# Start of a two-layer Fourier-filter network: filter weights in four pieces, the store of u in the next tick, image rows a tick earlier

## The chip, the cores and the metric

One Trainium2 chip, one of its cores. The metric is the device time of one execution in microseconds. The kernel before took 4927.3 us (median of three runs, 4927.09 to 4930.28).

## What is computed

Eight images of 128 x 128 points with 96 channels go through two layers. A layer is a convolution by Fourier transform, followed by a small network on every point.

```
x_pre = relu(x @ w1.T)**2 * scale + bias              # 96 -> 192 channels
xf    = rfft2(x_pre)                                  # over height and width
filt  = three small complex filters cw0, cw1, cw2, each enlarged
        to 128 x 65 by a matrix Rh on the left and Rw on the right
r     = softmax over the three filters, from means of x (one set per image)
xff   = xf * sum(filt * r)
xsp   = irfft2(xff) @ w2.T                            # 192 -> 96 channels
y     = feed-forward 96 -> 384 -> 96 with fp8 products, on each point
```

Two things matter here. The filters depend on the weights alone: the enlargement by Rw is done once per layer, early in the kernel, and its result `u` is kept in DRAM (`u_d`). The rest is done for every image.

## The kernel before

The program is written for one core and is entirely ordered by hand. Work is cut into generators: `pixels` (stage P, 21 steps) takes a group of eight image rows from load to width transform and stores it to `a_d`; `frequencies` (F, 19 steps) takes four columns of the spectrum, loads `al` from `a_d` and `ut` from `u_d`, makes the filter for the image (POOL multiplies `ut` by the gate, L703; PE makes `pf`, L715), multiplies and transforms back to `y_d`; `tokens` (S) does the rest and the feed-forward. `filters` (U) makes one of twelve parts of `u` for a layer; `Norms.steps` (N) finishes the statistics of normalisation; `gate` (G) computes the softmax of one image.

A tick is one pass over a list of triples (stage, step, ahead). In tick t the triple makes the named step for group t + ahead, less the offset of the stage. The order of a list is the order in which instructions stand on each engine. RAMP serves the ticks before 15, when only rows are worked on and the filters of layer 1 are made; RISE serves ticks 15 to 35, when spectra are worked on as well, and the filters of layer 2 are made in ticks 21 to 32; TICK serves the long steady part, FALL and TAIL the end. All DMAs are issued by SyncE (SP) in the order of the list, and SP waits for each one's inputs before it goes to the next.

What the change touches:

- `load_filters` (L279) issues the load of the filter weights `cw` of one layer, in four pieces of 26 partitions x 4608 values (468 KB each). It is called in `background`, a generator that advances by one yield per tick, after step 9 of P. For layer 1 that is in tick 0, for layer 2 in tick 17.
- `token_weights` (L408) loads and casts the feed-forward weights; `background` runs it for layer 1 in ticks 12 to 16.
- `filters` (L285) has three steps: four matmuls with `rw` (L292); two copies on ACT (L305); two copies on DVE (L307) together with the store of `u` to `u_d` (L311, 390 KB).
- `pixels` step 0 (L541 to L544) loads a group's rows into `xt` by four DMAs of 96 KB; step 1 takes its statistics on DVE (`st`, L483) and step 2 normalises it on POOL (`xn_a`, L554), which is the last reader. Three `xt` buffers rotate. In RAMP step 0 and step 1 both stand at ahead 4: a group is loaded in the tick in which its statistics are taken. In RISE and TICK the load stands at 3 and the statistics at 2.
- `padding` writes zeros between the halves of `u_d` (780 KB), in tick 11 for layer 1.
- RISE_GATE holds, by place in RISE, where gate steps are put in.

Shorter rows of names used below: `at` (L612, L613) is the width transform's result, stored to `a_d` at L616, 768 KB a tick; `xT` (L561) is the transposed group; `sd` (L587), `pa` (L596), `r` (L572), `xs` (L575) are steps between.

Of the kernel before, what the change touches and what calls it, by code (L numbers as in the profile page):

```python
# [10 lines left out]
F32 = mybir.dt.float32  # L11
# [8 lines left out]
B, H, W, C = 8, 128, 128, 96  # L20
# [53 lines left out]
}  # L74

RISE = (
    ("F", 7, 1), ("P", 1, 2), ("P", 0, 3), ("P", 13, -1), ("U", 0, 0), ("F", 12, 0),
    ("P", 3, 1), ("P", 5, 0), ("N", 0, 0), ("U", 1, 0), ("P", 4, 1), ("F", 13, 0),
    ("U", 2, 0), ("P", 14, -1), ("P", 6, 0), ("P", 15, -1), ("F", 8, 1), ("P", 16, -1),
    ("P", 17, -1), ("F", 14, 0), ("P", 7, 0), ("P", 18, -1), ("F", 9, 1), ("P", 8, 0),  # L80
# [20 lines left out]
)  # L101

RAMP = (
    ("U", 0, 0), ("P", 0, 4), ("P", 13, 0), ("U", 1, 0), ("P", 20, -1), ("P", 7, 1),
    ("P", 1, 4), ("U", 2, 0), ("P", 3, 2), ("P", 4, 2), ("P", 8, 1), ("N", 1, -1),
    ("P", 14, 0), ("N", 0, 0), ("N", 2, -1), ("P", 2, 3), ("P", 9, 1), ("P", 10, 1),
    ("P", 15, 0), ("P", 11, 1), ("P", 16, 0), ("P", 17, 0), ("P", 18, 0), ("P", 19, 0),
# [119 lines left out]
def _bc(ap, n):  # L227

    p, a = ap.shape
    return ap.unsqueeze(2).to_broadcast([p, a, n])  # L230
# [9 lines left out]
def metaformer_kernel(ctx: ExitStack, tc: tile.TileContext, x, cst, layers, out):  # L240
# [10 lines left out]
    def bank2(name):  # L251
        return pp.tile([128, 2, 512], F32, name=name, tag=f"d{banks[name]}")

    def bank1(name):
        return pp.tile([128, 512], F32, name=name, tag=f"s{banks[name]}")
# [23 lines left out]
    def load_filters(l, p):  # L279

        cws[l] = us.tile([128, UM, NG], F32, name="cw")
        for i in range(M // UM):
            nc.sync.dma_start(cws[l][32 * i : 32 * i + NWS], p["cw"][:, i * UM : (i + 1) * UM, :])

    def filters(i):  # L285

        l, n0 = i // NU, i % NU * UN
        pu = bank2("ps_u")
        pss = [pu[:NKW, i, : UN * UM] for i in range(2)]
        pss += [bank1(f"ps_v{i}")[:NKW, : UN * UM] for i in range(2)]  # L290
        for i in range(M // UM):
            mm(  # L292
                pss[i].rearrange("p (n m) -> p n m", m=UM),
                kt["rw"][32 * i : 32 * i + NWS],
                cws[l][32 * i : 32 * i + NWS, :, n0 : n0 + UN].rearrange("p m n -> p n m"),
                start=True,
                stop=True,
            )
        yield
        u = us.tile([NKW, UN, M], F32, name="u", bufs=3)  # L300
        uv = u.rearrange("p n (i m) -> p i n m", m=UM)
        for i, ps in enumerate(pss):
            o = ps.rearrange("p (n m) -> p n m", m=UM)
            if i < 2:
                nc.scalar.copy(uv[:, i], o)  # L305
            else:
                nc.vector.tensor_copy(uv[:, i], o)  # L307
            if i == 1:
                yield
        n1 = n0 if n0 < NHS else 64 + n0 - NHS  # L310
        nc.sync.dma_start(u_d[l][:, n1 : n1 + UN, :], u)  # L311
        yield
# [9 lines left out]
    def load(l, name, shape, view):  # L322
        temps[l][name] = us.tile(shape, F32, name=name)
        nc.sync.dma_start(temps[l][name], view)
        return temps[l][name]

    def kept(l, name, shape, dtype=F32):
        wts[l][name] = const.tile(shape, dtype, name=f"{name}_{l}")
        return wts[l][name]
# [78 lines left out]
    def token_weights(l, p):  # L408
        wt = wts[l]
        f1 = load(l, "f1_f", [C, HID], p["ffn_W1"])  # L410
        yield
        f2 = load(
            l, "f2_f", [128, HID // 128, C], p["ffn_W2"].rearrange("(k p) c -> p k c", p=128)
        )
        yield
        b1 = load(l, "b1_f", [128, HID // 128], p["ffn_b1"].rearrange("(k p) -> p k", p=128))
        b2 = load(l, "b2_f", [128, C], p["ffn_b2"].partition_broadcast(128))
        yield
        yield
        for name, t in (("f1", f1), ("f2", f2), ("b1", b1), ("b2", b2)):  # L420
            nc.vector.tensor_copy(kept(l, f"{name}_q", list(t.shape), F8), t, saturate=False)
        nc.vector.tensor_copy(kept(l, "b1", [128, HID // 128]), wt["b1_q"])
        nc.vector.tensor_copy(kept(l, "b2", [128, C], F16), wt["b2_q"])
        yield

    def background():

        load_filters(0, layers[0])
        constants("rw")
        yield  # L430
        yield from other_weights(0, layers[0])
        for k in ("fwd", "rh"), ("inv", "rh0"), ("fwd0", "inv0"), ("idft",):
            constants(*k)
            yield
        padding(0)
        yield
        yield from token_weights(0, layers[0])
        load_filters(1, layers[1])
        yield
        yield from projection_weights(1, layers[1])  # L440
        yield from other_weights(1, layers[1])
        yield from token_weights(1, layers[1])
# [14 lines left out]
    ab = ctx.enter_context(tc.tile_pool(name="ab", bufs=2))  # L457
# [79 lines left out]
    def pixels(jb, g):  # L537
        wt = jb.wt


        xt = ab.tile([128, 2, 2, 2 * C], F32, name="xt", bufs=3)  # L541
        for p in range(2):
            for a in range(2):
                nc.sync.dma_start(xt[64 * p : 64 * p + 64, a], pixel_rows(jb.src, g, p, a))  # L544
        yield
        if g == 0:
            jb.gs = ab.tile([C, NRG], F32, name="gs")
            jb.acc = ab.tile([128, 4, SC], F32, name="acc")
        xt = xt.rearrange("p a s (j c) -> p (a s j) c", c=C)
        nm = norms[-1].stats(0, xt)  # L550
        yield
        rs = nm.rs[:, 0]
        xn = ab.tile([128, RG, C], F32, name="xn_a")
        nc.gpsimd.tensor_tensor(xn, xt, _bc(rs, C), ALU.mult)  # L554
        yield
        pt = bank2("pt_a").rearrange("p a (r t) -> p (a r) t", t=128)[:C]
        for j in range(RG):
            nc.tensor.transpose(pt[:, j, :], xn[:, j, :], ident)  # L558
        yield
        xT = xTs[g % 2]  # L560
        nc.scalar.activation(xT[:C], pt, AF.Copy, accum_out=jb.gs[:, g : g + 1])  # L561
        yield
        sds = []
        for j in range(2):
            pw = bank2(f"pw{j}")[:, :, : 2 * WE]
            for a in range(2):
                for i in range(2):
                    o = pw[:, a, i * WE : (i + 1) * WE]
                    mm(o, xT[:, 4 * a + 2 * i + j, :], wt["w1"], start=True, stop=True)  # L569
            yield  # L570
            r = ab.tile([128, 2, 2, WE], F32, name="r")
            nc.scalar.activation(r.rearrange("p a s c -> p a (s c)"), pw, AF.Relu)  # L572
            yield
            xs = ab.tile([128, 2, 2, M], F32, name="xs")
            nc.scalar.activation(xs, r[:, :, :, :M], AF.Square)  # L575
            yield
            rc = r[:, :, :, M:].rearrange("p a s c -> p (a s) c")
            if g == 0 and j == 0:
                nc.gpsimd.tensor_copy(jb.acc, rc)
            else:  # L580
                nc.gpsimd.tensor_tensor(jb.acc, jb.acc, rc, ALU.add)  # L581
            yield

            sd = ab.tile([128, 2, 2, M], F32, name="sd")
            for e, op in enumerate((ALU.add, ALU.subtract)):
                on = nc.gpsimd if (j, e) in on_pool["sd"] else nc.vector
                on.tensor_tensor(sd[:, e], xs[:, 0], xs[:, 1], op)  # L587
            sds.append(sd)
            yield
        pas = []  # L590
        for j, sd in enumerate(sds):

            pa = bank2(f"pa{j}")[:, :, : 2 * M]
            for p in range(2):
                for e in range(2):
                    mm(  # L596
                        pa[64 * e : 64 * e + 64, p].rearrange("q (s m) -> q s m", m=M),
                        wt["dft"][64 * p : 64 * p + 64, 64 * e : 64 * e + 64],
                        sd[64 * p : 64 * p + 64, e],
                        start=True,  # L600
                        stop=True,
                    )
            pas.append(pa.rearrange("q p (s m) -> q p s m", m=M))
            yield

        at = ab.tile([128, RH, 2, M], F32, name="at")
        av = at.rearrange("q (p j) e m -> q p j e m", j=2)
        for j, pa in enumerate(pas):
            lo = ab.tile([128, 2, M], F32, name="lo")
            nc.scalar.copy(lo, pa[:, :, 1, :])  # L610
            yield
            nc.vector.tensor_tensor(av[:, :, j, 0, :], pa[:, :, 0, :], lo, ALU.add)  # L612
            nc.vector.tensor_tensor(av[:, :, j, 1, :], pa[:, :, 0, :], lo, ALU.subtract)  # L613
            if j == 0:
                yield
        nc.sync.dma_start(jb.a[:, g * RH : (g + 1) * RH], at)  # L616
        yield
# [388 lines left out]
    with tc.manual_schedule():  # L1006
# [5 lines left out]
        for t in range(-first, n + offset["S"] + behind + 1):  # L1012
# [23 lines left out]
            for place, (stage, step, ahead) in enumerate(order):  # L1036
                for gate_step, image in gates.get(place, ()):
                    advance("G", gate_step, image)
                i = t - offset[stage] + ahead
# [45 lines left out]
```

## Time and profile before

| | |
|---|---|
| median of the runs | 4927.3 us |
| profiled execution | 4929.2 us, span 4927.4 us, mean TensorE clock 0.986 |
| busy over the span | PE 4813.4, DVE 4592.9, ACT 4311.3, PE weight loads 3751.1, POOL 2532.6 us |
| DMA | 1020.97 MB, 207 GB/s |

The page gives the busy time of each engine over the whole span. The matmul time of PE is modelled, so a full PE is not a PE at its peak. The slices are 123 us long, longer than the whole ramp has dips; for a change at the start they have to be cut finer, with the table by stretches of time, whose columns are the length, the busy time of PE, PE weight loads, DVE, ACT and POOL (with counts), the granted clock, the DMA share and GB/s. In a list of waits, the three numbers are microseconds in total, how often, and the longest. In a timeline, a row has its start, its length, engine, line and operation; in brackets stands the idle time before it and what ended it.

### The profile page before, as it was taken

The numbers are of one execution on the slowest core, as the hardware profiler recorded it, in microseconds if no ns is written. First come the engines' busy times: TensorE is split into PE (matmuls) and PEld (weight loads), VectorE is DVE, ScalarE is ACT, GpSimd is POOL, SyncE is SP. The second block draws the span as 40 slices with busy tenths as digits, with TensorE's granted clock in tenths as the row PEclk, the third lists the DMA queues.
The fourth block names the chain that finished last, engine by engine and source line by source line (L and its number), as shares of the span: only waits on it lengthen the run. The fifth ranks groups of instructions, "written<-read, shape, count | busy, mean of one in ns | idle before, by whom it ended". The sixth has DMA issues, their size and how long they took to land.

```text
span 4927.4 us, 124008 instructions
## 1 busy us (share of the span) xinstructions
PE 4813.4 (98%) x44232; PEld 3751.1 (76%) x44232; DVE 4592.9 (93%) x13949; ACT 4311.3 (87%) x7104; POOL 2532.6 (51%) x1886
## 2 busy tenths in 40 slices
PE   7899999999999999999999999999999999999987
PEld 4677777777778777777777777777777877777763
DVE  7788999999999999999999999999999999998998
ACT  6555899999999999999999999999999999998987
POOL 4445455555555555555555555555555555554544
PEclk9899999999999999999999999999999999999997
DMA  5667777777777777777777777777777777776754
GB/s 174 189 196 196 208 213 217 215 213 214 213 215 217 213 215 212 219 208 219 212 216 213 214 214 213 217 216 214 214 212 215 219 211 215 211 218 182 204 168 126
DMA packets 917425, 1020.97 MB, mean 207 GB/s; under 512 B 75826, under 2 KB 848914, under 8 KB 916602
## 3 DMA queue, kind: packets, MB, share of 16 engines
q1 hardware_dynamic: 916810, 1013.04, 73.8%
q8 instruction: 353, 5.78, 0.5%
q14 instruction: 262, 2.15, 0.1%
HBM read 598.92 MB, written 413.84 MB: 206 GB/s over the span
## 4 chain that ended last, share of the span: by engine, by line
PE 88%; DVE 5%; ACT 4%; issue 1%; DMA 1%; SPq 1%; POOL 0%; POOLq 0%; DVEq 0%; ACTq 0%
PE pw L569 16%; PE py L749 14%; PE pz L839 8%; PE pf L715 7%; PE pa L596 7%; PE pi L855 7%; PE pm L934 6%; PE pz L831 5%; PE po L951 5%; PE pt_a L558 4%; PE ps_r L889 4%; PE pt_c L924 2%; DVE st L483 1%; ACT y L937 1%; ACT xn_c L910 1%
## 5 line engine op out<-in xcount | busy, mean ns | idle before, releaser
L792 POOL TENSOR_TENSOR xf<-pr 128x768 f32<-128x768 f32 x512 | 930.9, 1818 | 427.1 <-DVE pr L777 413.8
L569 PE MATMUL pw<-w,xT 97*128 97x240 f32 x4096 | 944.3, 374 | 7.4 <-DVE at L613 2.9
L749 PE MATMUL py<-k_fwd,al 128*128 128x128 f32 (+1 forms) x6208 | 801.9, 280 | 0.0
L937 ACT CAST y<-pm 128x1024 f16<-128x1024 f32 x768 | 754.8, 1017 | 42.8 <-PE pm L934 42.6
L569 PEld LDWEIGHTS pw<-w,xT 97*128 97x128 f32 x4096 | 742.5, 191 | 61.6 <-ACT r L572 7.4
L749 PEld LDWEIGHTS py<-k_fwd,al 128*128 128x128 f32 (+1 forms) x6208 | 744.5, 191 | 41.1 <-DVE pr L777 3.1
L944 ACT ACTIVATE h<-a 128x1024 fp8e5<-128x1024 f16 x729 | 773.1, 1061 | 0.2 <-DVE a L940 0.2
L969 POOL TENSOR_TENSOR y<-xr,o 128x768 f32<-128x768 f32 x256 | 421.9, 1648 | 674.1 <-DVE o L966 601.1
L581 POOL TENSOR_TENSOR acc<-acc,r 128x192 f32<-128x192 f32 x496 | 295.6, 596 | 919.5 <-ACT r L572 840.1
L572 ACT ACTIVATE r<-pw 128x960 f32<-128x960 f32 x512 | 496.9, 970 | 132.5 <-PE pw L569 131.2
L773 DVE TENSOR_TENSOR pr<-py,cf 128x768 f32<-128x768 f32 x512 | 486.3, 950 | 54.9 <-PE py L749 42.0
L587 DVE TENSOR_TENSOR sd<-xs 128x384 f32<-128x384 f32 x1008 | 518.7, 554 | 1.7 <-PE pa L596 1.4
L703 POOL TENSOR_TENSOR ut<-ut,rw 112x768 f32<-112x768 f32 (+1 forms) x256 | 473.2, 1849 | 49.8 <-DMA ut<-u_d 37.4
L715 PEld LDWEIGHTS pf<-k_rh,ut 48*128 48x128 f32 x6080 | 362.5, 189 | 159.4 <-issue 142.4
L934 PE MATMUL pm<-xq,f_q 96*128 96x512 fp8e5 x1536 | 431.9, 390 | 32.2 <-ACT y L937 25.2
L554 POOL TENSOR_TENSOR xn_a<-xt,n_rs 128x768 f32<-128x768 f32 x256 | 380.9, 1488 | 145.9 <-DVE n_rs L517 126.5
L927 ACT ACTIVATE xq<-pt_c 96x1024 fp8e5<-96x1024 f32 x256 | 260.7, 1018 | 202.8 <-PE pt_c L924 202.7
L575 ACT ACTIVATE xs<-r 128x768 f32<-128x768 f32 x512 | 436.6, 853 | 0.6 <-POOL sd L587 0.2
L715 PE MATMUL pf<-k_rh,ut 48*128 48x128 f32 x6080 | 412.4, 282 | 13.8 <-POOL ut L703 11.0
L910 ACT ACTIVATE xn_c<-xr,n_nb,n_rs 128x96 fp8e5<-128x96 f32 x1058 | 413.1, 488 | 0.0
L596 PE MATMUL pa<-sd,dft 64*64 64x384 f32 x4096 | 393.9, 496 | 8.9 <-DVE sd L587 6.2
L756 ACT COPY cf<-pf 128x768 f32<-128x768 f32 x496 | 372.7, 801 | 33.6 <-PE pf L715 33.2
(133 smaller groups left out, 10156.6 us busy)
## 6 DMA issues: line engine op xcount, KB each, us to landing
a_d<-at SPq DMA_DIRECT2D x256, 768.0 KB
al<-a_d SPq DMA_DIRECT2D x1024, 192.0 KB
y_d<-yt SPq DMA_DIRECT2D x512, 192.0 KB
v<-y_d SPq DMA_DIRECT2D x256, 384.0 KB
ut<-u_d SPq DMA_DIRECT2D x256, 336.0 KB
xt<-in_x_dram SPq DMA_DIRECT2D x512, 96.0 KB
xr<-in_x_dram SPq DMA_DIRECT2D x256, 192.0 KB
mid<-y SPq DMA_DIRECT2D x256, 192.0 KB
```

The source lines that it names most:

```text
L569: mm(o, xT[:, 4 * a + 2 * i + j, :], wt["w1"], start=True, stop=True)
L572: nc.scalar.activation(r.rearrange("p a s c -> p a (s c)"), pw, AF.Relu)
L587: on.tensor_tensor(sd[:, e], xs[:, 0], xs[:, 1], op)
L596: mm(pa[64 * e : 64 * e + 64, p].rearrange("q (s m) -> q s m", m=M), wt["dft"][64 * p : 64 * p + 64, 64 * e : 64 * e + 64], sd[64 * p : 64 ...
L703: nc.gpsimd.tensor_tensor(ut[:, -n:], ut[:, -n:], _bc_mid(jb.rw, n), ALU.mult)
L715: mm(pf[:, i, t * 128 : (t + 1) * 128], utf[64 * i : 64 * i + NHS, c0 : c0 + 128], kt["rh"][64 * i : 64 * i + NHS, :], start=True, stop=True,)
L749: mm(py[p0:p1, t, e, :], alf[:, e, c0 + p0 : c0 + p1], f, start=True, stop=True)
L773: nc.vector.tensor_tensor(p0, yv, crb, ALU.mult)
L792: nc.gpsimd.tensor_tensor(xf.rearrange("p t e f -> p (t e) f"), pr[:, 0].rearrange("p t r k -> p t (r k)"), pr[:, 1].rearrange("p t r k -> ...
L934: mm(pm[:, s, :], fk, xq[:, s, :], start=True, stop=True)
L937: nc.scalar.copy(y16, pm)
L944: nc.scalar.activation(hk, a16, AF.Copy, saturate=False)
```

## The change

The load of layer 2's `cw` yields between its four pieces. `background` starts it in the fourth step of layer 1's `token_weights`, so pieces are issued in ticks 15, 16, 17 and 18; layer 1's four pieces still go in one tick. What follows in `background` comes one tick later. The store of `u` becomes a fourth step of `filters`, which RAMP and RISE run as their first entry for the part of the tick before. RAMP loads rows at ahead 5 instead of 4, and `xt` has four buffers. As the first tick is numbered by the largest ahead in RAMP, the loop starts one tick earlier; that tick issues nothing.

```diff
 RISE = (
-    ("F", 7, 1), ("P", 1, 2), ("P", 0, 3), ("P", 13, -1), ("U", 0, 0), ("F", 12, 0),
+    ("U", 3, -1),    ("F", 7, 1), ("P", 1, 2), ("P", 0, 3), ("P", 13, -1), ("U", 0, 0), ("F", 12, 0),
...
 RAMP = (
-    ("U", 0, 0), ("P", 0, 4), ("P", 13, 0), ("U", 1, 0), ("P", 20, -1), ("P", 7, 1),
+    ("U", 3, -1), ("U", 0, 0), ("P", 0, 5), ("P", 13, 0), ("U", 1, 0), ("P", 20, -1), ("P", 7, 1),
...
         for i in range(M // UM):
+            if l and i:
+                yield
             nc.sync.dma_start(cws[l][32 * i : 32 * i + NWS], p["cw"][:, i * UM : (i + 1) * UM, :])
...
             if i == 1:
                 yield
+        yield
         n1 = n0 if n0 < NHS else 64 + n0 - NHS
         nc.sync.dma_start(u_d[l][:, n1 : n1 + UN, :], u)
...
-        load_filters(0, layers[0])
+        yield from load_filters(0, layers[0])
...
-        yield from token_weights(0, layers[0])
-        load_filters(1, layers[1])
+        cw1 = load_filters(1, layers[1])
+        for k, _ in enumerate(token_weights(0, layers[0])):
+            if k >= 3:
+                next(cw1)
+            yield
+        for _ in cw1:
+            yield
         yield
...
-        xt = ab.tile([128, 2, 2, 2 * C], F32, name="xt", bufs=3)
+        xt = ab.tile([128, 2, 2, 2 * C], F32, name="xt", bufs=4)
```

## The prediction

> **What bounds the kernel now.** I read the page's slices first, to see which stretches are not full.
>
> ```profile
> PE   7899999999999999999999999999999999999987
> PEclk9899999999999999999999999999999999999997
> ```
>
> One slice is 123 us. Apart from the end, PE and its clock dip only in the first two, so those were cut by stage, with TensorE's clock, the busy share of the DMA engines and GB/s last:
>
> ```profile
> 38.80:120.00 81.20, 73.96 (x468) 43.44 (x468) 68.12 (x250) 61.66 (x119) 37.92 (x39) 1.00 0.62 200
> 120.00:158.70 38.70, 33.53 (x191) 20.63 (x189) 28.39 (x106) 25.48 (x50) 15.98 (x18) 0.87 0.61 196
> 187.70:198.00 10.30, 2.61 (x17) 2.16 (x16) 4.22 (x10) 2.14 (x5) 0.03 (x1) 0.73 0.92 202
> 198.00:206.80 8.80, 6.97 (x46) 6.71 (x47) 7.21 (x17) 1.61 (x3) 5.51 (x4) 0.54 0.84 227
> 253.00:400.00 147.00, 146.29 (x1204) 110.59 (x1204) 123.19 (x326) 84.84 (x161) 72.08 (x56) 1.00 0.68 193
> 900.00:4500.00 3600.00, 3597.95 (x33859) 2849.92 (x33857) 3440.89 (x10405) 3304.38 (x5375) 1890.15 (x1401) 1.00 0.77 214
> ```
>
> From 900 to 4500 us PE (first pair) is busy 3598 of 3600 us: it sets the time, and the program's order there is the same in both kernels. So only the start can change. In 187.7 to 198 every engine stands and only the DMA engines work, 0.92 full; in the 8.8 us after it the clock is 0.54. The waits before 215 us say on what:
>
> ```profile
> DVE st L483 <- DMA xt<-in_x_dram: 24.6, 11, 6.8
> PEld pf L715 <- POOL ut L703: 11.8, 2, 9.9
> POOL ut L703 <- DMA ut<-u_d: 10.3, 1, 10.3
> ```
>
> VectorE waits eleven times for pixel rows, 24.6 us in all, and GpSimd once, for 10.3 us, for a filter tile. The timeline shows both places:
>
> ```profile
> 131.79 1.60 DVE L483 BATCH_NORM_STATS2 st<-xt 128x6 f32<-128x96 f32 x8 [4.90 <-DMA xt<-in_x_dram]
> 177.32 3.09 SPq L283 DMA_DIRECT2D cw<-in_L_cw_dram  x4
> 187.56 7.32 SPq L544 DMA_DIRECT2D xt<-in_x_dram  x4
> 197.97 1.80 POOL L703 TENSOR_TENSOR ut<-ut,rw 112x768 f32<-112x768 f32 x1 [10.30 <-DMA ut<-u_d]
> 199.82 2.93 PE L715 MATMUL pf<-k_rh,ut 48*128 48x128 f32 x24 [9.51 <-POOL ut L703]
> ```
>
> The four cw loads (4 x 468 KB) are issued at 177.3; ut, issued at 184.9, is not in before 198. One xT copy a tick gives the length of the ticks:
>
> ```profile
> 63.21 1.01 ACT L561 ACTIVATE xT<-pt_a 96x1024 f32<-96x1024 f32 x1
> 70.54 1.02 ACT L561 ACTIVATE xT<-pt_a 96x1024 f32<-96x1024 f32 x1
> 129.12 1.01 ACT L561 ACTIVATE xT<-pt_a 96x1024 f32<-96x1024 f32 x1
> 143.75 1.02 ACT L561 ACTIVATE xT<-pt_a 96x1024 f32<-96x1024 f32 x1 [0.28 <-PE pt_a L558]
> 170.13 1.02 ACT L561 ACTIVATE xT<-pt_a 96x1024 f32<-96x1024 f32 x1 [1.19 <-PE pt_a L558]
> 183.57 1.02 ACT L561 ACTIVATE xT<-pt_a 96x1024 f32<-96x1024 f32 x1 [1.57 <-PE pt_a L558]
> 206.78 1.02 ACT L561 ACTIVATE xT<-pt_a 96x1024 f32<-96x1024 f32 x1 [3.18 <-PE pt_a L558]
> ```
>
> A ramp tick takes 7.33 us where xt is in time (63.2 to 70.5) and 14.63 us where it is 4.9 us late (129.1 to 143.8); the cw tick takes 23.2 us, the one before it 13.4.
>
> [...] clock 0.54 after the 10 us stall, and 24 pf matmuls took 2.93 us against 1.54 at 445 us. So a long stall costs more than its length. [...] four xt issues, usually 2.5 us, took 7.32 behind cw. In both programs every issue also waits for the eighth issue before it to land, so one slow transfer holds the ones behind it. [...]
>
> **The change, part by part.**
>
> **xt a tick sooner (RAMP, four buffers).** Before, a row is issued at the head of the tick in which st reads it; SP reaches it only after the a_d and u stores of the tick before, and 2.3 to 2.8 us of transfer lie bare. After, it has a whole tick, 7 us or more. No instruction is added; two RISE ticks issue no xt instead of one. The fourth buffer keeps the load from waiting: with row t+5 issued in tick t it needs xn_a of row t+1, which ran two ticks back. What goes: the xt waits without that of the cw stall, 24.6 - 6.8 = 17.8 us. A second way: 14 ticks from 38.8 to 158.7 take 119.9 us; at 7.33 they would take 102.6, so 17.3 us less. This includes the padding write at 122.8 (780 KB, 4.9 us of wait and a cold clock after it): row 16 is now issued ahead of it. The cover of the loads is PE and DVE work, both near 7.3 us a tick; DVE is what waits, so most of the wait reaches the end. What is late next is the chain through PE, ACT and the shared PSUM banks: I take 15 of 17.5 us, bounds 8 and 18. Bytes: 384 + 768 + 390 KB in 7.33 us is 215 GB/s; the steady part moves 214, so it fits, closely.
>
> **Store of u a step of its own.** The 24 stores move behind the tick's small weight loads, to the head of the next tick, before xt in SP's order. SP had waited 33.5 us in twelve places for the copy at L307, with weight loads and xt behind it; the same wait now stands ahead of an xt load that has a tick to spare, and a_d behind that. Nothing waits for u soon: the last group of layer 1's filters is stored at the head of tick 15 and read at the end of tick 16; the three u buffers still return within three ticks. Counted at nothing by itself; without the earlier xt it would be worth under 1.5 us a tick, the issue time of two weight loads.
>
> **cw in four pieces.** Ticks 15 to 18 issue one piece each; before, tick 17 issued all four. Tick 18 took 23.2 us; without the stall I give it the 13.4 us of tick 17: 9.8 us less. The wait itself is 10.3 us, and the half clock behind it adds some 2.5 (pf 1.4, py 1.1), so 12.8 at most. Against that stand the pieces: 468 KB at 202 GB/s is 2.4 us each. Tick 17 then holds 384 + 768 + 468 + 768 + 336 KB = 2.79 MB, at 13.4 us 208 GB/s, about all that was seen; al and ut have one tick until they are read. In tick 16 there is no xt any more (384 KB) and a piece instead. I charge 3 us for one piece that shows: 10 us gained, bounds 0 and 13.
>
> **Shifted by it.** Layer 2's weight events come a tick later, still ahead of tick 36. The entry at the head of RISE shifts by one the places at which gate steps are put in; the order changes only in one late tick (416 to 435 us, gate of image 1): 0, bounds -1 and +1. One empty tick at the start issues nothing.
>
> **Sum**: -15 - 10 = -25 us. The profiled execution took 4929.2 us (span 4927.4 and 1.8 around it), the median of the runs is 4927.3. From the first 4904, from the second 4902; I say 4903. Bounds: -31 to -7, that is 4897 to 4921 with that middle shifted; both ends at once are unlikely.
>
> **The rivals.**
>
> *Only the cw part pays.* Another chain holds the ramp at 8.2 us a tick: at 109.8 to 121.3 the chain of waits runs ps_u, u, xs, xT, r, pa, without xt. Against it, three ticks of 7.3 with the same work. Gain 10 and a little: 4916.
>
> *Only xt pays.* The stall is spread over four ticks instead of removed. For it: the DMA share of 0.92. Gain 15: 4912.
>
> *Slower.* The pieces make al and ut late in each of ticks 16 to 19, and each wait is long enough to drop the clock: 4 x (w + 2.8). The gain of 25 is used up at w = 3.5 us; at w = 5, twice a piece's transfer, 31 us are lost: 4933. Against it: a tick of slack, and only one wait of the kind with four pieces at once.
>
> *Nothing.* The waits change name (r on PE, n_rs on ACT) and 4927 stays; the 4 us cold stretches alone make that unlikely.
>
> **How the numbers follow.** Both gains 0.71, only cw 0.09, only xt 0.09, nothing 0.05, slower 0.06. 0.2% is 9.9 us, about what a measurement of this kernel can tell from no change, so faster means under 4917.4. Of "only cw" I put a third on the side of no change: faster 0.84, same 0.09, slower 0.07. The likely case reaches from 4894 to 4914; with the two halves the range is 4893 to 4918.
>
> **What would show it.** Right: DVE's waits for xt before 215 us fall from 24.6 to under 5 us; xT copies every 7.3 to 7.6 us between 40 and 120; the tick after 129 us under 9; no wait of POOL at ut over 4 us; no stretch of clock 0.54 near 200 us; from 900 us on the same lengths. Wrong: ticks of 8.2 without xt waits; al, ut or pf waits in four neighbouring ticks; the forecast fails if the time is above 4918.

## The result and the profile after

| | before | after |
|---|---|---|
| median of six runs | 4928.44 us (4926.10 to 4932.13) | 4904.94 us (4902.51 to 4907.43) |
| profiled execution, span | 4929.20, 4927.4 us | 4904.48, 4901.7 us |

The ratio after to before is 0.9951, with a 95% interval from 0.9940 to 0.9961: 23.5 us faster. The forecast was 4903 us, in a range from 4893 to 4918.

The slices of the page after. The dips of PE and of the clock in the first two slices are nearly gone:

```profile
PE   8999999999999999999999999999999999999997
PEclk9999999999999999999999999999999999999997
```

The table by stretches of time, after (length; busy PE, PE loads, DVE, ACT, POOL; clock, DMA share, GB/s):

```profile
39.38:120.00 80.62, 78.88 (x520) 47.90 (x519) 76.30 (x277) 67.82 (x133) 42.97 (x44) 1.00 0.71 228
154.00:168.00 14.00, 10.84 (x81) 8.25 (x80) 10.98 (x39) 7.52 (x13) 5.31 (x4) 0.90 0.92 212
168.00:182.00 14.00, 11.85 (x88) 9.52 (x87) 12.27 (x27) 7.30 (x12) 7.97 (x6) 0.88 1.05 234
253.00:400.00 147.00, 145.94 (x1201) 109.92 (x1200) 123.71 (x328) 85.17 (x161) 71.84 (x56) 1.00 0.68 194
900.00:4500.00 3600.00, 3594.53 (x33816) 2846.51 (x33812) 3436.65 (x10397) 3299.71 (x5363) 1889.17 (x1397) 1.00 0.78 214
```

In the ramp PE is now busy 78.9 of 80.6 us and DVE 76.3, with 520 matmul instructions in the stretch instead of 468 in one of the same length. The stretch in which PE was busy for 2.6 of 10.3 us is gone; in its place are two ticks with a DMA share of 0.92 and 1.05 and PE at three quarters and more. (The share adds up the times of the packets that begin in a stretch, so it can pass 1.) The long stretch from 900 us is as before.

The waits of after up to 215 us. There is no row of DVE waiting for `xt` any more; of the waits at `ut` these are the largest left:

```profile
PEld pf L723 <- POOL ut L711: 4.1, 2, 2.2
POOL ut L711 <- DMA ut<-u_d: 2.6, 1, 2.6
```

The `xT` copies give the length of ticks. Of before, the fourth and the eighteenth:

```profile
38.82 1.00 ACT L561 ACTIVATE xT<-pt_a 96x1024 f32<-96x1024 f32 x1
...
158.71 1.02 ACT L561 ACTIVATE xT<-pt_a 96x1024 f32<-96x1024 f32 x1 [0.89 <-PE pt_a L558]
```

Of after, the same two with, between them, the two that answer to the 14.63 us tick of the padding; then those of ticks 17 and 18:

```profile
39.38 1.00 ACT L569 ACTIVATE xT<-pt_a 96x1024 f32<-96x1024 f32 x1
...
120.74 1.02 ACT L569 ACTIVATE xT<-pt_a 96x1024 f32<-96x1024 f32 x1
128.07 1.01 ACT L569 ACTIVATE xT<-pt_a 96x1024 f32<-96x1024 f32 x1
...
142.07 1.02 ACT L569 ACTIVATE xT<-pt_a 96x1024 f32<-96x1024 f32 x1 [0.90 <-PE pt_a L566]
...
154.36 1.02 ACT L569 ACTIVATE xT<-pt_a 96x1024 f32<-96x1024 f32 x1 [1.19 <-PE pt_a L566]
168.12 1.02 ACT L569 ACTIVATE xT<-pt_a 96x1024 f32<-96x1024 f32 x1 [1.57 <-PE pt_a L566]
182.34 1.02 ACT L569 ACTIVATE xT<-pt_a 96x1024 f32<-96x1024 f32 x1 [2.31 <-PE pt_a L566]
```

The tick with the padding takes 7.33 us, as most ticks of the ramp do, and the tick that took 23.2 us takes 14.2.

These copies make a ledger. The fourth copy comes at 38.82 us before and at 39.38 after; the eighteenth at 158.71 and 142.07: the ramp gives 16.6 us. The twenty-first comes at 206.78 and 182.34: another 7.8 us. Then the distance stays at 24.4 to 24.6 us up to 392 us, but for two copies in a row (25.4 and 24.9). Two later ticks differ by +1.6 and -1.6 us and cancel; at the end of the span it is 25.7.

### The profile page after: what moved, and what is told of

Read it like the earlier page. It is cut to its first block, busy times and chain, and to the rows that moved or that the text cites. A ratio compares the mean times of both kernels' runs of the same rounds, so it can differ in the third digit from the quotient of the medians.

```text
span 4901.7 us, 123978 instructions
## 1 busy us (share of the span) xinstructions
PE 4811.2 (98%) x44232; PEld 3752.2 (77%) x44232; DVE 4595.1 (94%) x13949; ACT 4314.8 (88%) x7104; POOL 2535.4 (52%) x1886
## 4 chain that ended last, share of the span: by engine, by line
PE 89%; DVE 5%; ACT 4%; issue 1%; DMA 0%; POOL 0%; SPq 0%; POOLq 0%; DVEq 0%; ACTq 0%
PE pw L577 17%; PE py L757 14%; PE pz L847 9%; PE pf L723 7%; PE pa L604 7%; PE pi L863 7%; PE pm L942 6%; PE pz L839 5%; PE po L959 5%; PE pt_a L566 5%; PE ps_r L897 4%; PE pt_c L932 2%; DVE st L491 1%; ACT y L945 1%; ACT xn_c L918 1%
## 5 line engine op out<-in xcount | busy, mean ns | idle before, releaser
L942 PE MATMUL pm<-xq,f_q 96*128 96x512 fp8e5 x1536 | 432.1, 391 | 28.7 <-ACT y L945 22.7
L847 PE MATMUL pz<-w2c,xf 128*128 128x96 f32 x2048 | 396.6, 275 | 0.0
```

The lines of the kernel that those rows point to most:

```text
L847: mm(pz[t][:, j, e, :], xf[:, 2 * t, e, :], wt["w2c" if t else "w2a"], start=False, stop=j == e == 1,)
L942: mm(pm[:, s, :], fk, xq[:, s, :], start=True, stop=True)
```

## The experiments

All are measured against the kernel before on the same chip. The ledger of all kernels, from the starts of the `xT` copies in each profile (fourth to eighteenth copy, ticks of RAMP and the first of RISE; eighteenth to twenty-first, in which the pieces of `cw` and the first `al` and `ut` meet; tick 36):

| kernel | 14 ticks of the ramp | next three | tick 36 | median, us |
|---|---|---|---|---|
| before | 119.9 | 48.1 | 19.5 | 4928.4 |
| after | 102.7 | 40.3 | 21.0 | 4904.9 |
| xt_only | 104.4 | 48.3 | 19.5 | 4915.1 |
| pieces_only | 120.0 | 37.0 | 17.9 | 4917.8 |
| ustore_only | 111.3 | 48.5 | 19.5 | 4923.0 |
| three_buffers | 106.1 | 38.1 | 17.9 | 4906.8 |
| group_tick15 | 104.4 | 43.7 | 21.0 | 4907.4 |
| early_padding | 104.4 | 39.8 | 17.9 | 4904.7 |
| late_pieces | 104.4 | 35.3 | 17.9 | 4909.7 |
| late_pieces_early_padding | 104.4 | 35.5 | 17.9 | 4908.4 |
| pieces_18_19 | 106.1 | 38.0 | 17.9 | 4902.1 |
| pieces_15_18_19 | 104.4 | 36.3 | 17.9 | 4900.1 |

The medians of before lay between 4929.0 and 4930.8 beside the experiments. The changed kernel's own median is from the measurement of the result, where before had 4928.4. The columns of ticks come from one profiled execution each, and the last section shows that such ticks can differ by 1.6 or 3.2 us with nothing changed in them.

**Rows a tick sooner, alone.**

```diff
-    ("U", 0, 0), ("P", 0, 4), ("P", 13, 0),
+    ("U", 0, 0), ("P", 0, 5), ("P", 13, 0),
-        xt = ab.tile(..., name="xt", bufs=3)
+        xt = ab.tile(..., name="xt", bufs=4)
```

> Only the rows a tick sooner with four buffers; cw and the store of u as before. Theory: the ramp's gain is the bare transfer of the rows, so the ramp falls to 7.33 us a tick (some 17 us from the fourth to the eighteenth xT copy) and the cw stall of about 10 us stays: 4909 to 4913 us. Rival (the earlier rows help only if SP reaches them sooner, with the store of u moved): ramp ticks stay near 8 us, 4920 us or more.

Measured: 4915.13 us, ratio 0.9969 (0.9956 to 0.9981), 2 us above the range that was expected. The ramp falls to 104.4 us. The waits of this kernel up to 215 us keep one row of DVE, and that is the `cw` stall, which is all there:

```profile
POOL ut L703 <- DMA xt<-in_x_dram: 10.8, 1, 10.8
DVE st L483 <- DMA xt<-in_x_dram: 7.5, 1, 7.5
```

The first row is the wait for `ut`, 10.3 us in before: POOL reads `ut` there and not `xt`. The profile infers the name from semaphores, of which all loads and stores use eight in turn: in the trace of before, each of the 4447 DMA issues that have an eighth issue ahead of them uses that one's semaphore. The earlier load alone takes the bare transfers away; SP does not need the store moved for that.

**Pieces of cw, alone.** The rest as before.

```diff
         for i in range(M // UM):
+            if l and i:
+                yield
...
-        load_filters(1, layers[1])
+        cw1 = load_filters(1, layers[1])
+        for k, _ in enumerate(token_weights(0, layers[0])):
+            if k >= 3:
+                next(cw1)
+            yield
...
```

> Only layer 2's cw in four pieces in ticks 15 to 18. Theory: the stall near 188 us goes, with its cold clock; ticks 16 to 18 grow by 1 to 2 us together: gain 7 to 10 us, 4918 to 4921 us, the ramp unchanged at 119.9 us for fourteen ticks. Rival (the stall moves): a wait of POOL at ut or of DVE at xt over 4 us elsewhere, gain under 3 us.

Measured: 4917.77 us, ratio 0.9975 (0.9966 to 0.9984), at the faster edge of what was expected. The ramp is unchanged, the three ticks after it fall from 48.1 to 37.0 us. In the waits up to 215 us the row of DVE loses its longest entry (6.8) and keeps the ramp's; POOL's wait at `ut` is short:

```profile
DVE st L490 <- DMA xt<-in_x_dram: 17.8, 9, 4.8
POOL ut L710 <- DMA ut<-u_d: 2.4, 1, 2.4
```

The 17.8 us are what the prediction computed for the ramp by subtraction. The stall does not come back elsewhere.

**Store of u, alone.**

```diff
+        yield
         n1 = n0 if n0 < NHS else 64 + n0 - NHS
         nc.sync.dma_start(u_d[l][:, n1 : n1 + UN, :], u)
...
-    ("F", 7, 1), ("P", 1, 2),
+    ("U", 3, -1),    ("F", 7, 1), ("P", 1, 2),
...
-    ("U", 0, 0), ("P", 0, 4),
+    ("U", 3, -1), ("U", 0, 0), ("P", 0, 4),
```

> Only the store of u as a step of its own at the head of the next tick (the gate's places in RISE shift with it). Theory: SP comes to xt earlier by at most the issue time of the tick's weight loads, under 1.5 us a tick in some ten ticks; gain 0 to 6 us, 4922 to 4928 us. Rival (the store was what held xt back): the ramp falls to near 7.33 us a tick, gain over 10 us.

Measured: 4922.99 us (4916.28 to 4929.86), ratio 0.9987 (0.9978 to 0.9995). The ramp loses 8.6 us, about half of what the earlier load takes: the tick of 9.94 us becomes 8.78, the one with the padding 11.48 instead of 14.63. DVE still waits ten times:

```profile
DVE st L484 <- DMA xt<-in_x_dram: 19.1, 10, 7.5
```

The store and the earlier load take away the same waits, so they do not add up: 104.4 us with the load alone, and 102.7 to 106.1 in the kernels that have both. The differences inside that band are in the first ticks: without the store moved (xt_only) the fourth to sixth copies lie 7.1 and 8.3 us apart, with it in pieces_18_19 and pieces_15_18_19 just so, in the changed kernel 6.4 and 7.4. No gain of the store beside the earlier load can be told from this.

**Three buffers.**

```diff
-        xt = ab.tile(..., name="xt", bufs=4)
+        xt = ab.tile(..., name="xt", bufs=3)
```

> The changed kernel with three xt buffers instead of four, rows still at ahead 5. Theory: the load in tick t then waits for xn_a of tick t-1 instead of t-2; POOL does that in the second half of the tick, so xt is issued late but still ahead of its use: 0 to 3 us slower than the changed kernel, 4904 to 4908 us. Rival (the fourth buffer carries the gain): xt waits of over 1 us a tick come back and the ramp takes 115 us or more for fourteen ticks, 4917 us or more.

Measured: 4906.84 us (4902.72 to 4907.80), ratio 0.9950 (0.9938 to 0.9963). One wait of DVE for `xt` comes back, near 47.8 us, when the first rows are loaded:

```profile
DVE st L491 <- DMA xt<-in_x_dram: 3.1, 1, 3.1
```

That tick takes 10.0 us. In the changed kernel it takes 7.4, but in every other kernel with earlier rows and four buffers 8.3. So the fourth buffer is worth 1.6 us at the start against those and 3.4 us in the ramp against the changed kernel, and in the medians no more than can be told.

**All four pieces in tick 15.**

```diff
         for k, _ in enumerate(token_weights(0, layers[0])):
-            if k >= 3:
-                next(cw1)
+            if k == 3:
+                load_filters(1, layers[1])
             yield
...
```

`load_filters` has no yields here, so the four loads go in one tick.

> The changed kernel with all four pieces of layer 2's cw in tick 15, two ticks sooner than before the change, not split. Theory (the amount in flight ahead of al and ut counts): 1.9 MB then stand ahead of a_d, al and ut of tick 16, some 9 us at 210 GB/s, and the tick that reads them waits: ticks 16 to 18 together 5 us or more longer than the 40.3 us of the changed kernel, 4909 to 4915 us. Rival (it only has to be out of tick 17, where xt, al and ut of the next ticks meet): within 2 us of the changed kernel.

Measured: 4907.44 us, ratio 0.9948 (0.9936 to 0.9961). The three ticks take 43.7 us, 3.4 more than in the changed kernel, less than the 5 expected. The stall comes back in small, one tick earlier; its timeline:

```profile
166.41 1.80 POOL L707 TENSOR_TENSOR ut<-ut,rw 112x768 f32<-112x768 f32 x1 [6.15 <-DMA xt<-in_x_dram]
167.74 1.38 DVE L487 BATCH_NORM_STATS2 st<-xt 128x6 f32<-128x96 f32 x8 [3.67 <-DMA xt<-in_x_dram]
168.27 2.93 PE L719 MATMUL pf<-k_rh,ut 48*128 48x128 f32 x24 [4.45 <-POOL ut L707]
```

So of the 7.8 us in these ticks of the profiles, 4.4 come from leaving tick 17, where no split is needed, and 3.4 from the split. The stall is there, but its price is not fixed: the other kernels with one piece in each of ticks 15 to 18 take 37.0 to 39.8 us, which would make it 3.9 to 6.7 us, while the medians lie 2.5 us apart and the ratios are 0.9948 and 0.9951, which tells nothing. Each theory was right in part.

**Padding ahead of tick 36.**

```diff
         yield from projection_weights(1, layers[1])
+        padding(1)
...
             if t == UEND:
-                padding(1)
```

> The changed kernel with layer 2's padding written in tick 25 instead of tick 36, where the loads of v and xr stand behind it. Theory: tick 36 loses the 6.8 us in which SP waits for that write; the tick of 21.0 us (17.9 to 21.0 in the runs so far) falls to about 15 us and its cold clock goes: gain 3 to 6 us, 4899 to 4902 us. Rival (v and xr wait for the pool's memory or for DMA bandwidth, not for the padding): under 1 us.

Measured: 4904.66 us (4899.51 to 4906.28), ratio 0.9942 (0.9928 to 0.9955): no different from the changed kernel. Tick 36 takes 17.9 us, and the three ticks after it take 17.4 to 18.2 in every kernel. My 15 us were wrong: from there on TICK is the order, and its tick is about 18 us long. All four kernels with an early padding have 17.9, and so have three of the eight others. The 1.6 or 3.2 us by which tick 36 is longer in the rest are not shown to be the padding's: PE stands for the same 1.8 us in that tick with either place of it, and three_buffers, with the padding where the changed kernel has it, takes 17.9 us at a granted clock of 1.00, the changed kernel 21.0 at 0.84 (last section). So no cost of the padding there is shown.

**Pieces in ticks 19 and 20.**

```diff
+        yield from token_weights(0, layers[0])
         cw1 = load_filters(1, layers[1])
-        for k, _ in enumerate(token_weights(0, layers[0])):
-            if k >= 3:
+        for k, _ in enumerate(projection_weights(1, layers[1])):
+            if k == 2:
                 next(cw1)
+                next(cw1)
+            if k == 3:
+                next(cw1)
+                next(cw1, None)
+            yield
...
```

> The changed kernel with the pieces of cw in ticks 19 and 20, two in each, instead of one in each of ticks 15 to 18; layer 2's other weights come two ticks sooner. Theory: ticks 16 to 18 have the DMA engines 0.92 to 1.0 busy with a piece in each, ticks from 19 on only 0.6 to 0.7 and are bound by PE, so the pieces hide there: ticks 16 to 18 fall from 40.3 to about 36 us, ticks 19 to 21 stay within 1 us: gain 2 to 4 us, 4901 to 4903 us. Rival (two pieces at once stall again): a wait at ut of 3 us or more in ticks 20 to 22 and no gain.

> Both: pieces of cw in ticks 19 and 20 and layer 2's padding ahead of tick 36. Theory: the two gains lie in different ticks and add up: 5 to 10 us under the changed kernel, 4895 to 4900 us. Rival: one of them is given back in the other's tick, 4901 us or more.

Measured: 4909.73 us (4905.49 to 4913.59) and, with the padding early as well, 4908.38 us (4906.46 to 4912.85). That is no gain over the changed kernel, where 2 to 4 us and 5 to 10 us were expected. Ticks 16 to 18 fell to 35.3 us as expected, but the tick that reads the filters grew from 15.9 to 22.7 us. The chain of waits of the first of the two says why. The last two pieces are issued at 203 us (the step before in the chain is a store to `y_d` of 9.3 us, which SP had to let land first, at 202.95) and land over 8 us later, with PE behind them:

```profile
202.96 1.02 SPq L285
...
204.03 8.27 DMA cw<-in_L_cw_dram
...
212.43 1.51 PE ps_v L294 x2
```

This was a wait that neither theory had named: the tick between the last piece and its first reader.

**Pieces one tick before that.** Both kernels have the padding early; pieces_18_19 has two pieces in tick 18 and two in 19, pieces_15_18_19 one in tick 15, one in 18 and two in 19. The second, against the changed kernel:

```diff
         for k, _ in enumerate(token_weights(0, layers[0])):
-            if k >= 3:
+            if k == 3:
                 next(cw1)
             yield
-        for _ in cw1:
-            yield
-        yield
-        yield from projection_weights(1, layers[1])
+        for k, _ in enumerate(projection_weights(1, layers[1])):
+            if k in (1, 2):
+                next(cw1)
+            if k == 2:
+                next(cw1, None)
+            yield
+        padding(1)
...
```

> The changed kernel with two pieces of cw in tick 18 and two in tick 19, and layer 2's padding ahead of tick 36. With the pieces in ticks 19 and 20 the matmuls of tick 21 waited for the last ones, issued late in tick 20. Theory: one tick more is enough: the tick of 22.7 us falls to 15.9, ticks 16 to 18 keep most of their gain (36 to 38 us against 40.3): 2 to 5 us under the changed kernel, 4899 to 4903 us. Rival (two pieces in tick 18 hold back its al and ut as before): a wait at ut of 3 us or more in tick 19 or 20, no gain.

> As the last, with one piece in tick 15, one in 18 and two in 19. Theory: tick 15 has no rows to load, so its piece is free; tick 18 carries one instead of two: ticks 16 to 18 at 36 to 38 us, 2 to 6 us under the changed kernel, 4898 to 4903 us. Rival: within 1 us of the changed kernel, because what is left in these ticks is the granted clock and not the transfers.

Measured: 4902.14 us (4900.41 to 4905.76) and 4900.05 us (4897.36 to 4901.54), ratios 0.9942 (0.9929 to 0.9956) and 0.9939 (0.9926 to 0.9951), both inside what was expected. In the first, ticks 16 to 18 take 38.0 us and the tick after them 15.7; in the second 36.3 and 14.3, and its reading tick 16.5. In the table by stretches of the second, the DMA share of the first two of these ticks is down to 0.6:

```profile
144.50:156.00 11.50, 7.79 (x51) 6.49 (x52) 7.37 (x30) 4.78 (x9) 2.83 (x2) 0.78 0.62 178
156.00:169.50 13.50, 10.34 (x80) 7.79 (x80) 10.74 (x37) 7.49 (x14) 5.31 (x4) 0.93 0.58 162
169.50:180.80 11.30, 10.80 (x90) 8.35 (x89) 9.56 (x27) 7.08 (x13) 6.87 (x6) 1.00 0.95 241
```

All its runs lie below all runs of the changed kernel, 4.9 us apart in the median, though the two were not measured together. The intervals of the two ratios overlap, since they carry the spread of the kernel before. It has the lowest median of all. What of that the pieces give is not separated from the clock, the cause that its rival names: tick 17 is as long as before (13.5 and 13.4 us) with a share of 0.58, and the clock was half for 6.8 us of ticks 16 to 18 against 13.7 in the changed kernel. pieces_only, with one piece in each tick and 6.8 us of half clock too, took 37.0 us there. Against that, the new places are 0.8 us shorter in the profiles.

## Why the prediction was right, point by point

- **Where the time can change.** Right. The ledger moves up to 182 us and hardly from there to 392; the steady stretch reads the same in both tables.
- **The ramp, 15 us.** 16.6 us measured, inside the bounds of 8 and 18: 17.2 between the fourth and the eighteenth copy, less 0.6 by which the fourth came later. The cause is confirmed by xt_only, where the same ramp falls by 15.5 us. That fourteen ticks came to 102.7 us where 102.6 had been worked out is partly luck: ten ticks are 7.3 us long, two of 8.2 are left at copies 9 to 11, and two of 6.4 and 6.7 make up for them. Six other kernels with the earlier rows have 104.4 us, 15.5 less than before. The sign "every 7.3 to 7.6 us" failed for the two ticks of 8.2.
- **Store of u, nothing by itself.** Not told apart from nothing beside the earlier load. Alone it gave 8.6 us in the ramp. Most ticks that gained, gained about 1 us, inside the bound of 1.5; the tick with the padding gained 3.2 us, twice that bound.
- **The fourth buffer "keeps the load from waiting".** True for the first rows only, 1.6 to 3.4 us; in the running ramp three would do, and the step should have said so, since `xn_a` of the tick before stands ahead of the load in either case.
- **cw in pieces, 10 us.** 7.8 us measured in this profile, inside the bounds of 0 and 13. Tick 18 gave 9.0 us of the 9.8; against it tick 16 grew from 11.4 to 12.3 us and tick 17 from 13.4 to 13.8. One profile does not fix the term. Three more kernels issue the same four pieces in the same ticks, and against the 48.1 us of before they gain 8.2 (early_padding), 10.0 (three_buffers) and 11.1 us (pieces_only). The clock read in three of the four goes with this: over these ticks it was half for 13.7 us in the changed kernel, 10.2 in three_buffers, 6.8 in pieces_only. The waits of tick 18 are alike, 2.2 to 2.7 us of POOL at `ut`. After it the 24 `pf` matmuls took 2.49 us in the changed kernel, where the clock was 0.50 for 3.4 us, and 1.61 in three_buffers, where it was 1.00 over the tick, as in pieces_only. So the charge of 3 us was fair, and what it left out is that a wait of 2.6 us, with PE idle for 1.84, was followed by half clock in the changed kernel. Its working had the transfer wrong: the bytes over 202 GB/s gave 2.4 us for a piece, but by the completion signals in the trace the four pieces of the changed kernel landed 6.7 to 7.7 us after their issue.
- **Gate places, 0.** The order in that tick changed and its time went from 18.45 to 16.89 us, but not for that reason: ustore_only has the shifted places and 18.5, pieces_only the old ones and 16.8. In before the clock is half for 3.4 us of that tick, and in the changed kernel it is full; the other two have the times of these.
- **The sum.** The ramp gave 1.6 us more than forecast and the pieces 2.2 less; that 25 us came so near to 23.5 owes something to this.
- **Sums and readings.** Why the stall has a DMA share of 0.92 at 202 GB/s where the ramp has 0.62 at 200 is not shown; in the trace each load of `cw` has thirteen completion signals at its landing, and a load of `xt` sixteen. The wait for the eighth issue before is in the trace: in before, `ut` was issued at 184.88 us as the eighth after the first load of `cw`, which had landed at 184.86, and it then took 13 us more with the other three loads ahead of it. None of the 4447 issues of before that have an eighth ahead of them began until that one had landed. The 24 `pf` matmuls at 445 us take 1.61 us in the view that has 2.93 for the slow ones (1.54 is from the view of the chain), so they lost 1.3 us and not 1.4. The parts of the chance of "faster" add up to 0.86, not 0.84.
- **The rivals.** "Only cw" fell with the ramp at 7.33, "only xt" with the stall that is gone. The slower one was a matter of degree: its mechanism is there, with 2.6 us of wait in one tick where 3.5 in each of four were needed; the 2.8 us of slower clock that it adds to each wait were the author's estimate. group_tick15 shows the mechanism at 6.1 us of wait, with 2.93 us for the `pf` matmuls behind it.

## What to carry to other kernels

Loads issued in the tick of their reader left their transfers bare here though the DMA share was only 0.62: in ten waits of up to 4.9 us each. A tick of lead removed that, and the buffer for it was needed only at the start. A bulk load is placed by looking at both ends: here four pieces in one tick held up the reads behind them by 10.3 us, and pieces issued in the tick before their first reader held up that reader, whose tick grew from 15.9 to 22.7 us. Where two edits remove the same wait, their gains measured one by one do not add: in the ramp the earlier rows gave 15.5 us alone and the store of u 8.6, and both together 13.8 to 17.2.

## What the runs showed of the hardware that was not expected

The same work differs from profile to profile by steps: tick 36 took 17.9 us in seven profiles, 19.5 in three and 21.0 in two, and the tick of the second image's gate 16.8 to 16.9 us in eight and 18.4 to 18.5 in four, also between kernels whose order there is equal. Where the granted clock was read, it goes with the steps. In tick 36 PE (TensorE) stands for 1.8 us until DVE has made `at`. The changed kernel and three_buffers there, first the matmuls after the pause, then the whole tick with its clock (0.84 and 1.00):

```profile
479.89 2.46 PE L577 MATMUL pw<-w,xT 97*128 97x240 f32 x8 [1.83 <-DVE at L621]
469.15:490.20 21.05, 19.22 (x142) 14.80 (x144) 17.00 (x50) 10.79 (x20) 8.06 (x6) 0.84 0.78 217
...
480.57 1.86 PE L577 MATMUL pw<-w,xT 97*128 97x240 f32 x8 [1.82 <-DVE at L621]
469.84:487.71 17.87, 16.05 (x142) 12.67 (x144) 17.11 (x50) 10.68 (x20) 8.09 (x6) 1.00 0.79 217
```

In before and in the changed kernel all changes of the clock lie a whole number of periods of 3.41 us apart, and these periods fall in different places of the two profiles. In the changed kernel the pause began 0.47 us into a period: two periods at half clock followed (481.0 to 487.8 us), and the tick took 21.0 us. In before it began 0.76 us into one: one period at half clock followed (506.4 to 509.8 us), 19.5 us. In three_buffers the clock stayed at 1.00, 17.9 us. So a pause of 1.8 us was followed by half clock in two of these profiles and not in the third. That the place of the pause in a period decides this fits the first two; it is not shown by them. The gate's tick took 18.45 us in before, with one such period in it (431.3 to 434.7 us), and 16.89 in the changed kernel, where the clock was 1.00. These steps of 1.6 and 3.2 us in the time are as large as some of the edits here, so an effect of that size is not to be read from one profile each.

In the ramp the 16 DMA engines moved 228 GB/s with a share of 0.71, and up to 243 GB/s between 120 and 142 us; the prediction had taken 208 GB/s for about all that was seen and 215 for a close fit.
